# A graph layer's sender rows: 36 of 3224 gathers replaced by row loads on SyncE's queue

## Chip, core, metric

The kernel runs on one core of a Trainium2 chip. The metric is the device time of one execution in microseconds, the median of several. The engines are called PE (TensorE), DVE (VectorE), ACT (ScalarE), POOL (GpSimd) and SP (SyncE) in the profile.

## What is computed

One attention layer of a graph network over 12,500 nodes and 412,500 edges, the edges sorted by receiver:

```
h = max(layernorm(x), 0)
for each edge e from s to d:
    msg_in   = [h[s], h[d], edge_attr[e]]                # 64 + 64 + 32
    message  = silu(msg_in @ W1 + b1) @ W2 + b2
    logit    = silu(msg_in @ Wa1 + ba1) @ Wa2 + ba2
att        = softmax(logit) over all edges
aggregated = sum of att * message by receiver
out        = x + silu([h, aggregated] @ Wu1 + bu1) @ Wu2 + bu2
```

The part that matters here is h[s]: each edge needs a row of its sender, and senders are in no order.

## The kernel before

**Node stage.** The products of h with the sender's and the receiver's part of `[Wa1, W1]` are computed once for each node and stored in HBM as two tables of rows of 128 numbers, 512 bytes each: `ts_d` for senders, `tr_d` for receivers.

**Edge stage (`one_pass`).** The edges are cut into tiles of P = 128, and K = 8 tiles make a group of 1024 edges. There are NG = 403 groups, 3224 tiles. For a group g, `load(g)` does the following:

- eight indirect gathers on GpSimd (line 448), one for each tile: 128 rows of `ts_d`, one to each partition, into `gs`, a tile of 128 x 8 x 128 numbers. The numbers of the senders lie in SBUF in `src_sb`, with an edge's place in its tile as the partition. The pool `gather` has eight buffers of `gs`, so GpSimd can be eight groups ahead.
- for every fourth group (NQ = 4), edge attributes `eo` and receivers `db` for four groups at once, loaded on SyncE's queue (lines 457 and 460), and four window starts read into SyncE's registers (`registers`, line 435, a TENSOR_LOAD).
- two loads on SyncE's queue of the window of receivers' rows (line 467), at an address that comes from such a register. The windows `wins` have three buffers, which the matmuls of line 475 release.
- DVE builds a one-hot matrix of the receivers in `eo` (line 471), and PE multiplies it and the edge attributes with the window (line 475). That gives `pe`, the receivers' and the edges' part.

`begin(g)` adds `gs` to `pe` (line 480, one DVE operation over 128 x 1024) and takes the tanh on ACT (line 481). `end(g)` makes messages and logits of it (lines 491 to 502); some groups later the messages are weighted, summed by receiver and put into `sums`. The order is: `begin(g)`, then `load(g + 2)`, then `end(g)`; the summing of an earlier group is placed between these parts.

A call `pin(...)` keeps an instruction in the program's order on its engine. The DMAs of the edge stage are not pinned; a scheduler places them on their queue, and it adds all semaphores. Between groups 16 and about 120 the bias of the node update is computed along the way (`tile_bias`, `node_bias`, `tile_rest`, lines 310 to 360), which gives SyncE's queue further loads and stores.

**Node update.** After the last group, tiles of 1024 nodes are scaled, passed through the last layers and stored (lines 671 to 745).

The line that the change is about, and the one that consumes its result:

```python
                for j in range(K):
                    nc.gpsimd.indirect_dma_start(
                        out=gs[:, j, :], out_offset=None, in_=ts_d[:, :],
                        in_offset=bass.IndirectOffsetOnAxis(ap=src_sb[:, t + j:t + j + 1], axis=0))
...
                pin(nc.vector.tensor_tensor(gss[g], pes[g], gss[g], ALU.add))
```

Of the kernel before, what the change touches and what calls it, by code (L numbers as in the profile page):

```python
# [44 lines left out]
F32 = mybir.dt.float32  # L45
I32 = mybir.dt.int32
AF = mybir.ActivationFunctionType
ALU = mybir.AluOpType
AX = mybir.AxisListType
ENG = mybir.EngineType  # L50
# [3 lines left out]
P = 128  # L54
# [3 lines left out]
C = 2 * U  # L58
S1 = U + 1
K = 8  # L60
# [8 lines left out]
NQ = 4  # L69
NC = 8  # L70
TABLES = 4
EPS = 1e-5
NEG = -3.0e38
BIG = 3.0e38
# [5 lines left out]
WHY = "a receiver's number; windows past the last node are padded"  # L80


@with_exitstack
def gnn_kernel(ctx: ExitStack, tc: tile.TileContext, n_edges, x, src, dst, dst_row, first, edge,
               weights, out):
    nc = tc.nc
    NB = x.shape[0] // P
    T = src.shape[1]
    NG = T // K
    NP = NB * P  # L90
# [6 lines left out]
    ts_d = dram.tile([NP, C], F32, name="ts_d")  # L97
# [13 lines left out]
    part, at = {}, 0  # L111
# [43 lines left out]
    with tc.tile_pool(name="node1", bufs=1) as node1, \  # L155
# [23 lines left out]
        pin = tc.keep_in_program_order  # L179
# [15 lines left out]
        eps = node1.tile([P, 1], F32, name="eps")  # L195
        nc.vector.memset(eps, EPS)
        pin(nc.scalar.activation(node1.tile([P, 1], F32, name="spare"), eps, AF.Sqrt))
# [90 lines left out]
        for c, nn in chunks:  # L288
            tr = node.tile([P, CB, C], F32, name="tr")[:, :nn, :]
            for b in range(0, nn, 4):  # L290
                n = min(4, nn - b)
                pn = node_ps.tile([P, 4, C], F32, name="pn", bufs=4)
                for i in range(0, n, 2):
# [7 lines left out]
        pin(nc.scalar.dma_start(hT_d, hT))  # L301

    one_pass(tc, n_edges, locals())
    again = nc.values_load(wrong[0:1, 0:1], min_val=0, max_val=1,
                           skip_runtime_bounds_check_because="it is the outcome of a comparison")
# [57 lines left out]
def one_pass(tc, n_edges, v):  # L363
    nc = tc.nc
    NB, T, NG, NP, NT = (v[k] for k in ("NB", "T", "NG", "NP", "NT"))
# [3 lines left out]
    ts_d, tr_d, bq_d, xb_d, edge, dst_row = (  # L369
        v[k] for k in ("ts_d", "tr_d", "bq_d", "xb_d", "edge", "dst_row"))  # L370
# [8 lines left out]
    pin = tc.keep_in_program_order  # L379

    with ExitStack() as ctx:
# [25 lines left out]
        for w in wins:  # L407
            nc.vector.memset(w, 0.0)
            for r in range(2):
                rows = slice(WR + r * DE, WR + (r + 1) * DE)  # L410
                nc.vector.tensor_copy(w[rows, :, r, :], we[rows, None, :].to_broadcast([DE, 2, C]))
        with tc.tile_pool(name="work2", bufs=2) as work2, \
                tc.tile_pool(name="small", bufs=3) as small, \
                tc.tile_pool(name="pre_ps", bufs=AHEAD + 1, space=PSUM) as pre_ps, \
                tc.tile_pool(name="one_ps", bufs=1, space=PSUM) as one_ps:
            pes, gss, lgs, ps_, psums, sps, pps, ees, mts = ({} for _ in range(9))


            w2t_ps = one_ps.tile([P, 4, P], F32, name="mt")[:U, 0, :S1]
# [4 lines left out]
            nc.tensor.matmul(w2u_ps, w2t, wu1a, start=True, stop=True)  # L424
            for h in range(2):
                nc.vector.tensor_copy(w2u[:, h, :], w2u_ps)
            at_sp, at_lo, at_hi, bus = {}, {}, {}, {}


# [3 lines left out]
            def registers(g, engine, at, base=base_sb, top=NP - 1):  # L433
                n = min(NQ, NG - g)
                _, regs = nc.values_load_multi_w_load_instructions(
                    base[0:1, g:g + n], engines=[engine], min_val=0, max_val=top,
                    skip_runtime_bounds_check_because=WHY)
                for i in range(n):
                    at[g + i] = regs[i]

            def load(g):

                t = g * K
                if g % NQ == 0:
                    registers(g, ENG.SP, at_sp)
                gs = gss[g] = gather.tile([P, K, C], F32, name="gs")
                for j in range(K):
                    nc.gpsimd.indirect_dma_start(  # L448
                        out=gs[:, j, :], out_offset=None, in_=ts_d[:, :],
                        in_offset=bass.IndirectOffsetOnAxis(ap=src_sb[:, t + j:t + j + 1], axis=0))  # L450
                if g % NQ == 0:
                    n = min(NQ, NG - g) * E2
                    eo = work2.tile([P, NQ, E2], F32, name="eo")
                    db = work2.tile([WR, NQ, E2], I32, name="db")
                    for i in range(g, min(g + NQ, NG)):
                        ees[i] = eo[:, i - g, :], db[:, i - g, :]
                    nc.sync.dma_start(eo.rearrange("p g e -> p (g e)")[WR:, :n],
                                      edge[:, g * E2:g * E2 + n])
                    for r in range(2):
                        nc.sync.dma_start(  # L460
                            db.rearrange("p g e -> p (g e)")[r * R:(r + 1) * R, :n],
                            bass.AP(tensor=dst_row.tensor, offset=dst_row[r:r + 1, g * E2:].offset,
                                    ap=[[0, R], [1, n]]))
                eo, db = ees.pop(g)
                win = wins[g % WINS]
                for r in range(2):
                    nc.sync.dma_start(win[r * R:(r + 1) * R, :, r, :],
                                      tr_w[bass.ds(at_sp[g], R), :, :])
                for h in range(2):
                    e = slice(h * E2 // 2, (h + 1) * E2 // 2)  # L470
                    pin(nc.vector.tensor_scalar(eo[:WR, e], db[:, e], bj[:, g, h:h + 1], None,  # L471
                                                op0=ALU.is_equal))
                pe = pes[g] = pre_ps.tile([P, K, C], F32, name="pe")
                for q in range(H):
                    pin(nc.tensor.matmul(pe[:, 2 * q:2 * q + 2, :], eo[:, q * P:(q + 1) * P],  # L475
                                         win[:, q // 2, :, :], start=True, stop=True))

            def begin(g):

                pin(nc.vector.tensor_tensor(gss[g], pes[g], gss[g], ALU.add))  # L480
                pin(nc.scalar.activation(pes[g], gss[g], AF.Tanh))  # L481

            def end(g):
# [99 lines left out]
            at, weighed = [None, None], [0]  # L583
# [28 lines left out]
            for g in range(AHEAD):  # L612
                load(g)
            done = 0
            for g in range(NG):
# [3 lines left out]
                if more and g == NG - 1:  # L619
                    next(more)  # L620
                begin(g)
                if more and g < NG - 1:
                    next(more)
# [8 lines left out]
                if g + AHEAD < NG:  # L632
                    load(g + AHEAD)
# [37 lines left out]
        with tc.tile_pool(name="upd1", bufs=1) as upd1, \  # L671
# [12 lines left out]
                                         engines=[ENG.SP, ENG.DVE, ENG.PE, ENG.Activation])  # L684
# [63 lines left out]
def general(tc, n_edges, v, dst):  # L748
# [7 lines left out]
    with ExitStack() as ctx:  # L756
        keep = ctx.enter_context(tc.tile_pool(name="keep_g", bufs=1))
        act_d = dram.tile([P, T, S1], F32, name="act_d")
        sum_d = [dram.tile([NP + P, S1], F32, name=f"sum_d{r}") for r in range(TABLES)]
        before = keep.tile([P, P], F32, name="before")  # L760
# [15 lines left out]
        rows = (NP + P) // P  # L776
        for r in range(TABLES):
            flat = sum_d[r].rearrange("(p b) f -> p (b f)", p=P)
# [66 lines left out]
        with tc.tile_pool(name="sums_g", bufs=2) as work, \  # L845
                tc.tile_pool(name="sums_g_ps", bufs=2, space=PSUM) as sums_ps:
            for g in range(0, T, G):
# [3 lines left out]
                for k in range(0, ng, K):  # L851
# [26 lines left out]
                    for j in range(K):  # L878
                        nc.gpsimd.indirect_dma_start(
                            out=sum_d[(t + j) % TABLES][:, :],  # L880
                            out_offset=bass.IndirectOffsetOnAxis(ap=to[:, j:j + 1], axis=0),
# [6 lines left out]
        with tc.tile_pool(name="upd_g", bufs=2) as work, \  # L888
                tc.tile_pool(name="upd_g_ps", bufs=2, space=PSUM) as upd_ps:
            for c in range(0, NB, CB):  # L890
                part = work.tile([P, TABLES, CB, S1], F32, name="part")
                for r in range(TABLES):
                    nc.sync.dma_start(part[:, r], sum_v[r][:, c:c + CB, :])
                for r in range(1, TABLES):
                    nc.vector.tensor_tensor(part[:, 0], part[:, 0], part[:, r], ALU.add)
# [95 lines left out]
```

## Time and profile before

| What | Value |
|---|---|
| median of 3 runs | 4154.89 us (4154.44 to 4157.52) |
| profiled execution, device time | 4154.71 us |
| its span, first to last instruction | 4153.0 us |
| granted TensorE clock, mean | 0.638 of full speed |
| first gather starts / last gather ends | 50.8 us / 4082.75 us |
| DMA queue of GpSimd: packets, MB, share of 16 engines | 103168, 211.49, 20.4% |
| DMA queue of SyncE: packets, MB, share of 16 engines | 107538, 168.42, 15.4% |

The profile shows one execution. A group line gives the source line, the engine, the operation, output and inputs with shapes and the count; then the total busy time in us and the mean duration in ns; then the idle time of the engine just before these instructions, and what ended most of it. "issue" is time in which the engine waited for nothing that the profile shows. The line of tenths cuts the span into 40 slices; a digit is the busy share of that slice, so 7 is 70%. A timeline line starts with the start and the length in us. SPq is SyncE's queue: its instructions issue DMAs and don't count as busy.

### The profile page before, as it was taken

What the parts mean: (1) busy time and instruction counts of PE and PEld (TensorE: products, weight loads), DVE (VectorE), ACT (ScalarE), POOL (GpSimd) and SP (SyncE); (2) the same over time, 40 slices, a digit from 0 to 9 for tenths busy, and PEclk for the clock granted to TensorE, in tenths of its full rate; (3) what the DMA queues carried; (4) which work ended last, traced back from release to release, by engine and by line L of the source; (5) the groups of instructions that cost most, each with busy time, mean ns of one, the idle gap of its engine ahead of it and who ended that gap; (6) DMA issues with size and microseconds to landing.
All of it is one profiled execution on the core that took longest, in us unless ns stands there. A gap on an engine that the chain in (4) does not pass through costs nothing.

```text
span 4153.0 us, 45361 instructions
## 1 busy us (share of the span) xinstructions
PE 2227.8 (54%) x10980; PEld 1802.9 (43%) x10980; DVE 2986.2 (72%) x8482; ACT 584.9 (14%) x1235; POOL 3065.0 (74%) x3249
## 2 busy tenths in 40 slices
PE   5555554545555555545555555555554555655555
PEld 4433443434444444444444444444443444444445
DVE  6867776767677677776777767777677776777777
ACT  3211111111111111111111111111111111111112
POOL 3777777777777777777777777777777777777773
PEclk8666666766666556666666666666666566556665
DMA  7433343434333333333333333333333333333323
GB/s 276 109 86 96 98 102 97 102 92 107 97 90 88 90 81 90 83 87 90 80 90 83 88 90 80 90 82 88 90 80 90 82 88 90 81 90 82 88 77 112
DMA packets 212354, 392.54 MB, mean 95 GB/s; under 512 B 73009, under 2 KB 137842, under 8 KB 198898
## 3 DMA queue, kind: packets, MB, share of 16 engines
q0 software_dynamic: 103168, 211.49, 20.4%
q1 hardware_dynamic: 107538, 168.42, 15.4%
q10 hardware_dynamic: 1376, 9.67, 0.6%
q8 instruction: 90, 1.47, 0.1%
q14 instruction: 182, 1.49, 0.1%
HBM read 363.56 MB, written 25.72 MB: 94 GB/s over the span
## 4 chain that ended last, share of the span: by engine, by line


## 5 line engine op out<-in xcount | busy, mean ns | idle before, releaser
L448 POOL DMA_INDIRECT gs<-ts_d,src_sb x3224 | 3047.9, 945 | 1032.5 <-issue 932.2
L475 PE MATMUL pe<-wins,eo 128*128 128x256 f32 x3224 | 1421.7, 616 | 1080.7 <-DVE eo L471 953.5
L475 PEld LDWEIGHTS pe<-wins,eo 128*128 128x128 f32 x3224 | 954.6, 311 | 1370.9 <-DVE eo L471 1025.2
L480 DVE TENSOR_TENSOR gs<-pe,gs 128x1024 f32<-128x1024 f32 x403 | 491.6, 1220 | 942.5 <-DMA gs<-ts_d,src_sb 932.1
L481 ACT ACTIVATE pe<-gs 128x1024 f32<-128x1024 f32 x403 | 413.9, 1027 | 2487.2 <-DVE gs L480 1776.1
L543 DVE TENSOR_SCALAR wt<-iota_w,dloc,p 128x40 f32<-128x40 f32 x3224 | 719.1, 316 | 0.1
L549 PE MATMUL sp<-wt,acts 128*65 128x40 f32 x6448 | 608.4, 267 | 0.7 <-DVE wt L543 0.7
L549 PEld LDWEIGHTS sp<-wt,acts 128*65 128x65 f32 x6448 | 578.6, 183 | 1.1 <-DVE wt L543 0.8
L560 PEld LDWEIGHTS mt<-ss,w2u 65*128 65x128 f32 x806 | 221.4, 289 | 495.9 <-issue 446.6
L560 PE MATMUL mt<-ss,w2u 65*128 65x40 f32 x806 | 184.9, 324 | 386.0 <-DVE gm L526 381.3
L499 DVE TENSOR_TENSOR pe<-pe,w_all 128x512 f32<-128x512 f32 x403 | 281.6, 699 | 12.6
L491 DVE SCALAR_TENSOR_TENSOR acts<-pe,gs 128x512 f32<-128x512 f32 x403 | 277.7, 689 | 15.5 <-ACT pe L481 5.2
L497 DVE SCALAR_TENSOR_TENSOR pe<-pe,gs 128x512 f32<-128x512 f32 x403 | 280.2, 695 | 10.9
L471 DVE TENSOR_SCALAR eo<-db,bj 64x256 f32<-64x256 int32 x806 | 280.0, 379 | 7.6
L502 DVE TENSOR_REDUCE lg<-pe 128x8 f32<-128x512 f32 x403 | 276.5, 686 | 8.9
L519 PE MATMUL mt<-ident,mx 128*128 128x128 f32 x103 | 44.8, 435 | 409.4 <-DVE sums L577 360.6
L519 PEld LDWEIGHTS mt<-ident,mx 128*128 128x128 f32 x103 | 18.3, 178 | 420.1 <-issue 417.7
L579 DVE COPY stand<-nmax 64x40 f32 x806 | 151.5, 188 | 2.0
L530 ACT ACTIVATE scale<-fall 128x1 f32<-128x1 f32 x103 | 20.9, 203 | 804.8 <-DVE fall L529 804.8
L577 DVE TENSOR_TENSOR sums<-sums,mt 64x40 f32 x600 | 113.4, 189 | 28.7 <-PE mt L560 24.0
L555 ACT COPY ss<-sp 65x40 f32<-65x40 f32 x403 | 73.6, 183 | 21.4 <-PE sp L549 20.4
L573 DVE SCALAR_TENSOR_TENSOR sums<-sums,scale,mt 64x40 f32 x206 | 52.4, 254 | 33.2 <-PE sp L549 23.3
(91 smaller groups left out, 565.4 us busy)
## 6 DMA issues: line engine op xcount, KB each, us to landing
gs<-ts_d,src_sb POOLq DMA_INDIRECT x3224
eo<-in_edge_dram SPq DMA_DIRECT2D x100, 512.0 KB
db<-in_dst_row_dram SPq DMA_DIRECT2D x200, 256.0 KB
wins<-tr_d SPq DMA_DIRECT2D x806, 32.0 KB
ts_d<-ts SPq DMA_DIRECT2D x5, 896.0 KB
tr_d<-tr ACTq DMA_DIRECT2D x5, 896.0 KB
hT_d<-hT ACTq DMA_DIRECT2D x1, 3136.0 KB
hb<-hT_d SPq DMA_DIRECT2D x48, 64.0 KB
```

Source lines behind the costliest of these rows:

```text
L448: nc.gpsimd.indirect_dma_start(out=gs[:, j, :], out_offset=None, in_=ts_d[:, :], in_offset=bass.IndirectOffsetOnAxis(ap=src_sb[:, t + j:t ...
L471: pin(nc.vector.tensor_scalar(eo[:WR, e], db[:, e], bj[:, g, h:h + 1], None, op0=ALU.is_equal))
L475: pin(nc.tensor.matmul(pe[:, 2 * q:2 * q + 2, :], eo[:, q * P:(q + 1) * P], win[:, q // 2, :, :], start=True, stop=True))
L480: pin(nc.vector.tensor_tensor(gss[g], pes[g], gss[g], ALU.add))
L481: pin(nc.scalar.activation(pes[g], gss[g], AF.Tanh))
L491: pin(nc.vector.scalar_tensor_tensor(acts[g % ACTS][:, :, 0:U], th[:, :, U:C], 1.0, gs[:, :, U:C], op0=ALU.add, op1=ALU.mult))
L497: pin(nc.vector.scalar_tensor_tensor(att, th[:, :, 0:U], 1.0, gs[:, :, 0:U], op0=ALU.add, op1=ALU.mult))
L499: pin(nc.vector.tensor_tensor(att, att, wa2[:, None, :].to_broadcast([P, K, U]), ALU.mult))
L502: pin(nc.vector.tensor_reduce(lgs[s][:, k:k + K], att, AX.X, ALU.add))
L543: pin(nc.vector.tensor_scalar(wt[:, j, :], iota_w[:, j // H, :], dloc[:, g * K + j:g * K + j + 1], p[:, k + j:k + j + 1], op0=ALU.is_equal ...
L549: pin(nc.tensor.matmul(sp, acts[g % ACTS][:, j, :], wt[:, j, :], start=j == 0, stop=j == K - 1))
L560: pin(nc.tensor.matmul(pp, w2u.rearrange("s h u -> s (h u)"), sps.pop(g), start=True, stop=True))
```

## The change

On 36 groups (11, 22, up to 396) GpSimd gathers seven tiles rather than eight. The eighth tile's 128 rows are fetched one by one, as 128 plain loads of 512 bytes on SyncE's queue, into a tile of their own, `alone[g]` (two buffers). Twelve rows are issued in each of the eleven `load` steps ahead of the group (eight in the last). The row numbers come from a new input, `src_row`, the list of senders as one row in HBM: 128 of them are loaded to one partition (`numbers`), and twelve are read into SyncE's registers in each step. In `begin` the add for such a group is made in two operations, over 128 x 896 and over 128 x 128.

```diff
+QUEUES = [(ENG.SP, 11, 0, 12)]
...
+            rows_at, rows_to = {}, {}
+            dma = {ENG.SP: nc.sync, ENG.Activation: nc.scalar}
+
+            def numbers(q, g):
+
+                if g < NG - 4:
+                    t = g * K + K - 1
+                    rows_at[q, g] = small.tile([1, P], I32, name=f"one_src{q}", bufs=2)
+                    nc.sync.dma_start(rows_at[q, g], v["src_row"][:, t * P:(t + 1) * P])
+
+            def rows(q, g):
+                engine, every, phase, n_rows = QUEUES[q]
+                if g == 0:
+                    numbers(q, phase + every)
+                if g < phase:
+                    return
+                at = (g - phase) % every
+                g = g - at + every
+                if at == 0:
+                    rows_at.pop((q, g - every), None)
+                    if (q, g) in rows_at:
+                        alone[g] = work2.tile([P, C], F32, name=f"one_gs{q}")
+                if at == every // 2:
+                    numbers(q, g + every)
+                if (q, g) not in rows_at:
+                    return
+                a = at * n_rows
+                n = min(n_rows, P - a)
+                if n <= 0:
+                    return
+                load, regs = nc.values_load_multi_w_load_instructions(
+                    rows_at[q, g][0:1, a:a + n], engines=[engine], min_val=0, max_val=NP - 1,
+                    skip_runtime_bounds_check_because=WHY)
+                for k in range(n):
+                    dma[engine].dma_start(alone[g][a + k:a + k + 1, :], ts_d[bass.ds(regs[k], 1), :])
...
@@ load(g)
-                for j in range(K):
+                for j in range(K - (g in alone)):
                     nc.gpsimd.indirect_dma_start(
...
                                       tr_w[bass.ds(at_sp[g], R), :, :])
+                for q in range(len(QUEUES)):
+                    if QUEUES[q][0] == ENG.SP:
+                        rows(q, g)
...
@@ begin(g)
-                pin(nc.vector.tensor_tensor(gss[g], pes[g], gss[g], ALU.add))
+                n = K - (g in alone)
+                pin(nc.vector.tensor_tensor(gss[g][:, :n, :], pes[g][:, :n, :], gss[g][:, :n, :], ALU.add))
+                if n < K:
+                    pin(nc.vector.tensor_tensor(gss[g][:, n, :], pes[g][:, n, :], alone.pop(g), ALU.add))
                 pin(nc.scalar.activation(pes[g], gss[g], AF.Tanh))
...
+        "src_row": padded(src, t * P)[None],
```

More of the change, by code (lines that the diff above doesn't have):

```diff
@@ L83, in gnn_kernel @@
 @with_exitstack
-def gnn_kernel(ctx: ExitStack, tc: tile.TileContext, n_edges, x, src, dst, dst_row, first, edge,
+def gnn_kernel(ctx: ExitStack, tc: tile.TileContext, n_edges, x, src, src_row, dst, dst_row, first, edge,
                weights, out):
@@ L415, in one_pass @@
                 tc.tile_pool(name="one_ps", bufs=1, space=PSUM) as one_ps:
-            pes, gss, lgs, ps_, psums, sps, pps, ees, mts = ({} for _ in range(9))
+            pes, gss, lgs, ps_, psums, sps, pps, ees, mts, alone = ({} for _ in range(10))
             w2t_ps = one_ps.tile([P, 4, P], F32, name="mt")[:U, 0, :S1]
```

## The prediction

> **What bounds the kernel now.** I read the busy shares first, then the costliest groups, then the waits of GpSimd alone between 130 and 4083 us, then the timeline at the end of the gathers. The busy shares leave it open (VectorE 72%, GpSimd 74%); the group lines begin to decide.
>
> ```profile
> PE 2227.8 (54%) x10980; PEld 1802.9 (43%) x10980; DVE 2986.2 (72%) x8482; ACT 584.9 (14%) x1235; POOL 3065.0 (74%) x3249
> ...
> POOL 3777777777777777777777777777777777777773
> ...
> L448 POOL DMA_INDIRECT gs<-ts_d,src_sb x3224 | 3047.9, 945 | 1032.5 <-issue 932.2
> ...
> L480 DVE TENSOR_TENSOR gs<-pe,gs 128x1024 f32<-128x1024 f32 x403 | 491.6, 1220 | 942.5 <-DMA gs<-ts_d,src_sb 932.1
> ```
>
> 3224 gathers of 945 ns, each with a gap ahead of it that is put down to "issue", which is a wait for nothing. VectorE's idle time is nearly all at L480, waiting for the gathers to land. The waits of GpSimd (what it waited for, us in total, times, longest) say that no other engine holds it up:
>
> ```profile
> POOL gs L448 <- issue: 867.3, 2846, 0.3
> POOL gs L448 <- DVE eo L471: 32.0, 105, 0.3
> POOL gs L448 <- DMA gs<-ts_d,src_sb: 31.4, 103, 0.3
> POOL gs L448 <- DVE gs L480: 18.6, 61, 0.3
> ```
>
> The longest is 0.3 us, the ordinary gap, whoever is named as releaser. So after the start GpSimd never waits for a buffer: it runs at its own pace. The timeline gives that pace and its end:
>
> ```profile
> 4080.56 0.94 POOL L448 DMA_INDIRECT gs<-ts_d,src_sb  x1 [0.30 <-issue]
> 4081.81 0.94 POOL L448 DMA_INDIRECT gs<-ts_d,src_sb  x1 [0.30 <-issue]
> 4106.60 1.26 POOL L710 TENSOR_TENSOR uT<-uT,bu_in 128x512 f32<-128x512 f32 x1 [23.84 <-DVE uT L705]
> ```
>
> One gather every 1.249 us (median start to start over the whole trace; the mean from the first at 50.8 to the last at 4081.8 is 1.251). A group of eight takes 9.99 us. The last gather ends at 4082.75, and 70.25 us of tail follow to 4153.0.
>
> The other queue that matters is SyncE's, which is to carry the new work: its waits in total, then the durations (ns, min/median/max) of the two lines that resemble the new instructions, and one pair in the timeline.
>
> ```profile
> SPq L467 <- PE mt L560: 1266.4, 199, 12.4
> SPq L467 <- PE pe L475: 800.9, 107, 10.4
> SPq L460 <- DVE wt L543: 748.3, 97, 18.9
> SPq L467 <- PE sp L549: 458.8, 94, 11.8
> ...
> L435 SPq TENSOR_LOAD <-base_sb x101: 294/298/1808, 78.8 to 4013.5; - x101
> ...
> L467 SPq DMA_DIRECT2D wins<-tr_d x806: 316/317/1368, 86.3 to 4041.0; - x162
> ...
> 1992.32 0.82 SPq L467 DMA_DIRECT2D wins<-tr_d  x2
> ```
>
> SyncE waits about 3270 us of the span in these four lines alone, mostly for one of the three window buffers to come free. Two window loads take 0.82 us from first start to second end; less 0.317, a load with a register in its address costs 0.50 us start to start, address arithmetic included.
>
> **What the Trainium skill says.** "DMA: Bandwidth & Descriptors", section "Issuing engines are not separate DMA queues": DMAs from SyncE, ScalarE and GpSimd end on the same 16 engines, and spreading them saves only the issuing sequencer's time. That time is exactly what is short here: the two main queues take 20.4% and 15.4% of the 16 engines, while GpSimd issues without a pause. The same page, "Why a DMA increments its semaphore by 16 and not by 1", advises one semaphore for each transfer in flight. The trace agrees: SyncE's loads rotate over eight semaphores, and the records show each load waiting for the one eight before it to land. Its "Latency and other measured facts" puts a tensor_load at some 600 ns at least; here four registers take 298 ns, and the measurement decides.
>
> **Removed.** Targets are groups 11, 22, ... 396: the list of senders is fetched only for a group below NG - 4 = 399, so there are 36, as the title says. Each drops one gather: 36 x 1.249 = 45.0 us of GpSimd's time. All of it lies on the path, since GpSimd never pauses for 0.3 us or more between 130 us and its end. Unless something below becomes late, its last gather moves from 4082.75 to 4037.8, and the tail (unchanged code) with it.
>
> **Added on SyncE.** One turn of 11 groups lasts 11 x 9.99 = 109.9 us before and 108.7 us with one gather fewer. Into it go 128 row loads and 11 register loads, plus one 512-byte list load.
> - A row load: 0.50 us, as a window load, since it also takes its address from a register. Lower end 0.36 us (317 ns and its 45 ns gap, arithmetic free); upper end 0.65, since the strided loads of L318 and L355 take 598 and 656 ns (medians). I take 0.50: a row is simpler than a window, 512 bytes rather than 32 KB. 128 x 0.50 = 64 us.
> - A register load: 12 numbers rather than 4. At best one of 0.35 us (298 ns and its gap), at worst three; 11 x 0.35 = 4 us, up to 12. The list load 0.4 us.
> - What SyncE does already: per group two window loads (1.0 us), a quarter of the eo, db and register loads (0.43), and on average 0.2 for the node bias, with semaphore instructions some 1.85 us (704 us active between 200 and 4000 us, summed from the records). 11 x 1.85 = 20 us.
> - Rotation of semaphores: eight rows back is 4.0 us at 0.50 each. A window load lands 1.75 us after issue (median from the records), so rows don't wait for rows; an eo load lands after 5.0 us and a db load after 3.9 (6.1 in the slowest tenth), so a row eight behind one waits 1 to 2 us, three times in four groups at most: up to 7 us a turn.
>
> Sum: 64 + 4 + 0.4 + 20 + 7 = 95 us of 108.7; with three register loads 103. SyncE fits, at 88 to 95%.
>
> **What is queued behind the rows.** The rows of a step stand after that step's two window loads, so the next windows come up to 6 us later, and behind them the matmul L475, then L480. What covers this: from the records a window load is issued 25.9 us (median; 17.4 at the fifth percentile) ahead of its matmul, eo 47.9 us ahead. And because SyncE runs ahead of TensorE by the three buffers and mostly waits for it, the rows fill that wait rather than add to it. If SyncE is late for longer, VectorE gets late; GpSimd still has eight gather buffers, some 60 us, before it stops. The register loads stayed behind the window loads of the preceding group in the records, so I expect the rows to keep their place too, and not to be drawn forward in one burst of 128. The densest stretch is 200 to 1250 us, where the node bias adds 0.7 us per group instead of 0.2: about 100 us a turn, near the limit, but the slack covers it.
>
> At the start, step 0 loads its list and waits for it on SyncE (some 2 us), then issues 12 rows (6 us) ahead of the second window. GpSimd starts at 50.8 and VectorE's first add is at 98.5, so five groups of lead cover that: nothing.
>
> **Added on VectorE.** The add of 128x1024 (1220 ns) becomes 128x896 and 128x128. Rows of those shapes take 1093 (L231) and 281 ns (L728): +0.15 us, and up to four more semaphore instructions of 50 ns since the rows came on eight semaphores: 0.35 x 36 = 13 us. VectorE waits 932 us for gathers, so this costs nothing; without that cover it would cost the 13 us. The rows' landing is no new wait: the last eight rows are issued with the step before the target's own window, more than 17 us ahead of the target's matmul.
>
> **Added on the DMA engines.** 4608 rows of 512 bytes, 2.4 MB beside 392.5 MB. If each is cut in 16, that is 74,000 packets beside 212,354: perhaps 10% more of engines that are a third busy. Gathers may land a little later; their pace is GpSimd's, so nothing.
>
> **Sum.** 4154.71 (this execution; span 4153.0 and 1.7 around it) - 45.0 = 4109.7; the median of the runs, 4154.89, is 0.2 above this execution. Forecast 4110 us.
>
> **The rivals.**
> - Partly lost (4118 to 4146, as a point 4130): in the dense stretch SyncE falls behind for longer than the slack, windows come late, and VectorE stalls until the stretch is over. For it: 100 of 108.7 us there, and SyncE's own waits in order (it waits for the x transfer and VectorE's add before L360). Against: VectorE needs 7.2 busy us per group of 9.96 and catches up. Chance 0.07.
> - No change (4155): VectorE is really what paces, in bursts. For it: pairs of groups without a pause. Against: GpSimd's waits never exceed 0.3 us. 0.02.
> - Slower: SyncE becomes the bound. It decides from the row price at which its turn exceeds 109.9 us: (109.9 - 20.4 - 4.3) / 128 = 0.67 us, or 0.61 if the semaphore waits come to 7 us. At 0.70 us a turn takes 20.4 + 4.3 + 89.6 = 114.3, so 36 x 4.4 = 158 us more: 4313. For it: no load of one row is in the trace, twelve in a row follow each other without a pause, which no line of SyncE does now, and loads at L318 cost 0.6. Against: those move 64 partitions in several runs, and the second of a window pair costs 317 ns like the first. 0.11.
>
> **How the numbers follow.** The main case has 0.80, most of it between 4104 and 4118; the spread being the few us by which the end of the groups and the tail can fall differently. With the lower part of the partial case, 4104 to 4132 holds 8 in 10. A measurement here can tell about 0.2%, 8.3 us, from no change: faster 0.86 (main, nearly all of the partial case), same 0.03, slower 0.11.
>
> **What would show it.** Right: 3188 gathers at the same 1.249 us with no wait of GpSimd over 0.3 us, the last ending near 4038, a tail of 70 us, rows about 0.50 us apart, SyncE still waiting at L467. Wrong: matmuls at L475 waiting for windows, GpSimd waiting for VectorE at a group's start, rows over 0.6 us apart, or a longer gap between gathers.

## The result, and the profile after

| | before | changed |
|---|---|---|
| median, us | 4155.69 (4 runs) | 4114.97 (4 runs) |
| ratio, 95% interval | | 0.9902 (0.9885 to 0.9919) |
| profiled execution, span | 4153.0 | 4113.8 |
| gathers | 3224 | 3188 |
| last gather ends, then tail | 4082.75, 70.2 | 4043.2, 70.6 |

The kernel before took 4152 to 4158 us beside most of the runs below and 4155 to 4167 us beside four of them, so every run is compared, by ratio, with the kernel before that ran beside it.

The change gains 40.7 us by the medians and 39.2 us between the two profiled spans; the forecast was 45.0 us and 4110 us, with a range of 4104 to 4132. The page's lines for GpSimd and for two VectorE groups after the change, and then the second of these groups before it:

```profile
POOL 3777777777777777777777777777777777777773
...
L487 POOL DMA_INDIRECT gs<-ts_d,src_sb x3188 | 3018.7, 947 | 1022.1 <-issue 952.1
...
L523 DVE TENSOR_TENSOR gs<-pe,gs 128x1024 f32<-128x1024 f32 (+1 forms) x403 | 487.7, 1211 | 775.5 <-DMA gs<-ts_d,src_sb 740.0
...
L513 DVE TENSOR_SCALAR eo<-db,bj 64x256 f32<-64x256 int32 x806 | 259.7, 360 | 158.6 <-DMA db<-in_dst_row_dram 151.5
```

```profile
L471 DVE TENSOR_SCALAR eo<-db,bj 64x256 f32<-64x256 int32 x806 | 280.0, 379 | 7.6
```

GpSimd still sets the pace, with 36 gathers fewer, and a mean gather of 947 rather than 945 ns. VectorE waits less for gathers (740 us against 932), but it has a new wait: 151.5 us for `db`, whose loads stand in SyncE's queue (before, all idle time at that line was 7.6 us). The three largest waits of GpSimd between 130 and 4044 us say that this reaches it nowhere:

```profile
POOL gs L487 <- issue: 887.3, 2910, 0.3
POOL gs L487 <- DMA gs<-ts_d,src_sb: 14.0, 46, 0.3
POOL gs L487 <- DVE eo L513: 14.0, 46, 0.3
```

As before, no wait is longer than 0.3 us. SyncE's side: its waits, the durations (ns, min/median/max) of the new register loads, and a stretch of its timeline.

```profile
SPq L506 <- PE pe L517: 291.7, 69, 9.9
SPq L506 <- PE mt L605: 256.1, 138, 10.8
SPq L506 <- PE sp L594: 99.0, 84, 5.2
...
SPq L464 <- DMA db<-in_dst_row_dram: 88.9, 118, 1.4
```

```profile
L460 SPq TENSOR_LOAD <-one_src x396: 527/933/1367, 88.6 to 3933.3; - x198
```

```profile
2014.12 0.86 SPq L506 DMA_DIRECT2D wins<-tr_d  x2
2016.15 4.82 SPq L464 DMA_DIRECT2D one_gs<-ts_d  x12
2021.88 0.86 SPq L506 DMA_DIRECT2D wins<-tr_d  x2
```

At the window loads, some 2530 us of waiting before have shrunk to 650 at L506; the 748 us before that for the buffers of `db` are nearly gone too (24.9 us, now at L496). Between the window pair and the first row lies the register load of 0.93 us; twelve rows take 4.82 us, 0.41 us from one to the next (median). In the records SyncE is active for 79% of the time between 200 and 4000 us. Active means here, and below, its instructions with the gaps between them, where a gap is no longer than 0.4 us.

### The profile page after: what moved, and what is told of

Same layout as the page of the kernel before. It is cut to its first block, busy times and chain, and to the rows that moved or that the text cites. A ratio compares the mean times of both kernels' runs of the same rounds, so it can differ in the third digit from the quotient of the medians.

```text
span 4113.8 us, 59789 instructions
## 1 busy us (share of the span) xinstructions
PE 2284.8 (56%) x10980; PEld 1852.9 (45%) x10980; DVE 3021.4 (73%) x8518; ACT 584.3 (14%) x1235; POOL 3035.8 (74%) x3213
## 2 busy tenths in 40 slices
DMA packets 220602, 393.50 MB, mean 96 GB/s; under 512 B 77077, under 2 KB 146554, under 8 KB 207034
## 4 chain that ended last, share of the span: by engine, by line
## 5 line engine op out<-in xcount | busy, mean ns | idle before, releaser
L517 PE MATMUL pe<-wins,eo 128*128 128x256 f32 x3224 | 1477.3, 638 | 967.7 <-DVE eo L513 819.6
L517 PEld LDWEIGHTS pe<-wins,eo 128*128 128x128 f32 x3224 | 1000.5, 325 | 1265.8 <-DVE eo L513 970.2
L523 DVE TENSOR_TENSOR gs<-pe,gs 128x1024 f32<-128x1024 f32 (+1 forms) x403 | 487.7, 1211 | 775.5 <-DMA gs<-ts_d,src_sb 740.0
L588 DVE TENSOR_SCALAR wt<-iota_w,dloc,p 128x40 f32<-128x40 f32 x3224 | 734.0, 320 | 0.1
L513 DVE TENSOR_SCALAR eo<-db,bj 64x256 f32<-64x256 int32 x806 | 259.7, 360 | 158.6 <-DMA db<-in_dst_row_dram 151.5
L624 DVE COPY stand<-nmax 64x40 f32 x806 | 163.4, 203 | 0.6
```

The costliest lines, as they stand in the source:

```text
L523: pin(nc.vector.tensor_tensor(gss[g][:, :n, :], pes[g][:, :n, :], gss[g][:, :n, :], ALU.add))
L588: pin(nc.vector.tensor_scalar(wt[:, j, :], iota_w[:, j // H, :], dloc[:, g * K + j:g * K + j + 1], p[:, k + j:k + j + 1], op0=ALU.is_equal ...
```

## The experiments

### Is the gain the gathers, and are the rows free?

**Gathers dropped, no rows** (the 36 tiles' sender rows and the loads of their numbers are left out; the add takes zeros).

```diff
...
-                    if (q, g) in rows_at:
-                        alone[g] = work2.tile([P, C], F32, name=f"one_gs{q}")
+                    if g < NG - 4:
+                        alone[g] = v["zero"]
...
-                if (q, g) not in rows_at:
-                    return
+                return
```

> The 36 eighth gathers are left out and nobody fetches these rows: the add takes zeros for them, in the same two VectorE operations; no row load, no list load. Theory A (the gain is GpSimd's pace times the gathers removed, and the rows are hidden on SyncE; the 5 us that the changed kernel lacks come from gathers that are stretched now and then while VectorE works, whoever fetches the rows): 4155.7 - 36 x 1.25 = 4110.7, with up to 5 us more if gathers are stretched here too, so 4111 to 4116, within 0.15% of the changed kernel. Rival B (the rows' traffic or SyncE's lateness costs the 5 us): 4110 to 4111 with no more stretched gathers than in the kernel before, and a clear 4 to 5 us below the changed kernel.

**Rows loaded, gathers kept** (the eighth gather's result is overwritten by the second add).

```diff
-                for j in range(K - (g in alone)):
+                for j in range(K):
```

> The rows are loaded as in the changed kernel and added as there, but GpSimd gathers all eight tiles too (its eighth result is overwritten by the add). Theory A: as before, 4155 to 4160, GpSimd at 1.25 us per gather, no wait over 0.3 us. Rival B (rows slow the gathers by traffic): 4160 to 4162. Rival of the forecast (SyncE sets the pace with these rows): clearly slower than before, over 4170.

**The changed kernel once more.**

> The changed kernel once more, on the same chip as the two above. 4112 to 4117; a repeat of the profile should again show some 70 gathers of over 960 ns if these are fixed by the program's order, and another number if they are chance.

| Run | ratio to before | interval | span of the profiled execution | gathers over 960 ns |
|---|---|---|---|---|
| gathers dropped | 0.9906 | 0.9891 to 0.9921 | 4113.5 | 68 |
| rows, gathers kept | 1.0007 | 0.9999 to 1.0015 | 4165.7 | 59 |
| changed again | 0.9901 | 0.9886 to 0.9917 | 4113.1 | 77 |

The kernel without the rows is not faster than the one with them, and the rows without the saving cost at most 0.15%. So the gain is the dropped gathers, and 4608 row loads are hidden, in this amount. Rival B falls: the 5 us are missing where no row is loaded, too. So does the forecast's rival of no change: VectorE does not set the pace, since fewer gathers alone give the gain. The span of the second run is longer mostly because all of GpSimd ran at a median of 1.252 us from gather to gather in that execution, rather than 1.249; the kernel before was slower beside it, too.

### Where the missing 5 us are

From the records, gathers over 960 ns exceed the usual 944 by 5.5 us in all in the kernel before (60 gathers) and by 9.6 us in the changed kernel (72); the rest of the shortfall is spread thinly over the pace. Of the long ones in the changed kernel, 23 start at the same place in VectorE's order (26 in its repeat). One of them in the timeline:

```profile
2729.55 0.60 DVE L513 TENSOR_SCALAR eo<-db,bj 64x256 f32<-64x256 int32 x2
2729.83 1.19 POOL L487 DMA_INDIRECT gs<-ts_d,src_sb  x1 [0.30 <-issue]
...
2730.08 0.20 DVE L651 SCALAR_TENSOR_TENSOR total<-total,scale,psum 128x1 f32<-128x1 f32 x1
2730.21 1.76 DVE L588 TENSOR_SCALAR wt<-iota_w,dloc,p 128x40 f32<-128x40 f32 x8
```

The gather takes 1.19 us instead of 0.94; it starts with the second L513, and the add to `total` and the building of `wt` follow. Before the change there were only four in that place. So this place alone makes 4.6 us of the difference. Two runs move that add behind the building of `wt`, in the changed kernel and in the kernel before:

```diff
+                    by_node(g)
                     if g == starts[s]:
                         pin(nc.vector.scalar_tensor_tensor(total, total, scale[:, s:s + 1],
                                                            psums.pop(s), op0=ALU.mult, op1=ALU.add))
-                    by_node(g)
```

> The changed kernel with VectorE's addition to total (128x1) placed behind the eight operations that build wt, instead of ahead of them, in the first group of each batch. Theory S (gathers are stretched by about 0.24 us where they begin with a fixed run of VectorE operations, total among them): the gathers over 960 ns in that place vanish or change in number, 4 to 6 us at most, ratio 0.989. Rival (stretching has nothing to do with VectorE's order): again 20 to 30 such gathers and the same time.

> The kernel before, without the change, with the addition to total behind the building of wt. Theory S: before the change few gathers met that run (four or five, 1 us in all), since groups and gathers stood in one fixed phase; so 1 us at most, ratio 0.999 to 1.000. If it gains 5 us here too, what the order of total brings has nothing to do with the change.

The changed kernel goes to 0.9887 (0.9872 to 0.9902), its profiled span to 4104.7. Its gather line in the groups:

```profile
L487 POOL DMA_INDIRECT gs<-ts_d,src_sb x3188 | 3010.9, 944 | 1022.1 <-issue 927.5 <-DMA gs<-ts_d,src_sb 50.9 <-DVE gs L523 13.1
```

The mean is 944 ns; 24 gathers exceed 960 ns, none of them in that place, and the busy time falls by 7.8 us, a little more than the 4 to 6 us that were expected at most. The kernel before stays at 0.9994 (0.9986 to 1.0003). The two ratios of the changed kernel overlap in their intervals; what shows the effect is the gathers themselves. Within the changed kernel, too, the records hold a comparison: of the gathers that start less than 25 ns after a second L513, 23 of 28 are long where the add to `total` follows, and none of 63 where `wt` follows at once; with the add moved, none of 80. So this loss comes from VectorE's order meeting the gathers.

Why the change brings them together is open in part. Before, the add to `total` mostly stands at one place in the gathers' rhythm: 58 of 100 adds start 1.22 to 1.25 us after the last gather's start, 4 start 0.23 to 0.27 us after it, which is the bad place. In the changed kernel it is 27 and 28. Groups with seven gathers would shift this rhythm, but they can't be the whole reason: the run with the rows and all eight gathers has 25 adds in the bad place, and 24 long gathers there. That run and the one with the gathers dropped (31 long gathers there) have in common the add made in two operations, which makes VectorE's order longer in 36 groups; no run has that alone.

Why this run of instructions holds a gather is argued only: the Trainium skill, "SBUF — State Buffer", section "SBUF: two separate sides", says that a VectorE operation in a mode that uses both of its ports locks GpSimd out of the shared pair, so that it cannot write descriptors, and "Who interferes with whom" counts tensor_scalar among the operations that can enter such a mode. L513 and L588 are tensor_scalar, though no trace here shows their mode; and of the 838 gathers that overlap an L588 in the changed kernel, 775 take 960 ns or less. So the page gives a direction, not the case.

### How far SyncE can carry it

**44 tiles, 15 rows per step**, the same code with other numbers:

```diff
-QUEUES = [(ENG.SP, 11, 0, 12)]
+QUEUES = [(ENG.SP, 9, 0, 15)]
```

> Every ninth group, 15 rows per step, 44 tiles rather than 36. SyncE's sum for a turn of nine groups: 128 rows x 0.412 + 128 registers x 0.08 + 9 x 1.85 + 1 = 81 us, with waits for semaphores some 85, against 88.7 us that GpSimd takes. Theory A: it still fits, 4155.7 - 44 x 1.25 + 5 = 4106. Rival (SyncE near its limit already costs, and more rows give part of it back): 4115 or above, with matmuls waiting for windows.

Ratio 1.0893 (1.0878 to 1.0908): slower by 370 us, far beyond theory A's 4106 us and beyond what its rival had in mind (4115 or above). The waits and the register load of this run:

```profile
DVE eo L513 <- DMA db<-in_dst_row_dram: 1032.1, 97, 22.0
...
PE pe L517 <- DMA wins<-tr_d: 773.4, 164, 12.7
```

```profile
L460 SPq TENSOR_LOAD <-one_src x396: 531/3178/3667, 88.4 to 4378.1; - x198
```

VectorE and TensorE wait for loads of SyncE's queue, and SyncE is active for 99% of the time from 1300 to 4000 us. The surprise is the register load: 3.18 us in the median for 15 numbers, against 0.93 for 12. Split by step, it takes 3.26 us, but 1.55 and 1.64 us in the two of these steps whose first number lies at 0 and 60, multiples of four. (The ninth step reads the last 8 numbers, from 120, in 0.71 us.) Two runs separate the count from the start:

**44 tiles, 16 rows per step**, so that each start is a multiple of 16: `(ENG.SP, 9, 0, 16)`.

> Every ninth group again, 44 tiles, but 16 rows per step (8 steps with rows, the ninth without), so every register load starts at a multiple of 16 numbers. Theory L (the run with 15 rows was slow because of its register loads alone: 3.26 us where the first number lay at no multiple of four, 1.6 us where it did, against 0.93 for 12 numbers): a register load of 16 takes 1.2 to 1.6 us, SyncE's turn sums to 53 (rows) + 8 x 1.3 + 17 + 1 = 81 us of 88.7, GpSimd sets the pace again: ratio to before 0.987 to 0.989, 10 us faster than the changed kernel. Rival N (it is the number of rows per turn or loads of more than 12 numbers as such): register loads of 3 us again, ratio over 1.03.

**The changed kernel with its list one number further on**, 12 numbers per load as before:

```diff
-                    rows_at[q, g] = small.tile([1, P], I32, name=f"one_src{q}", bufs=2)
+                    rows_at[q, g] = small.tile([1, P + 4], I32, name=f"one_src{q}", bufs=2)[:, 1:P + 1]
```

> The changed kernel with its list of 128 row numbers stored one number further on in SBUF, so that no register load starts at a multiple of four numbers; 12 numbers per load as before. Theory L (the start decides): a register load takes 2.6 us or so rather than 0.93, SyncE's turn grows by 11 x 1.7 = 18 us to some 104 of 108.7, so the stretch of the node bias overflows and the gain is partly or wholly lost: ratio 0.995 to 1.02. Rival (the count of 15 did it): 0.93 us as before and ratio 0.990.

The register loads of the two, in this order:

```profile
L460 SPq TENSOR_LOAD <-one_src x352: 973/1157/1602, 89.0 to 3962.5; - x176
```

```profile
L460 SPq TENSOR_LOAD <-one_src x396: 1673/2654/3082, 88.9 to 3999.9; - x198
```

16 numbers from a start at a multiple of four take 1.16 us, 12 from one number further on 2.65. The start decides, as theory L has it. And it decides the result: the changed kernel with nothing but this shift is slower than before, 1.0065 (1.0050 to 1.0081).

The other half of theory L's expectation for the 44 tiles failed: 1.0003 (0.9995 to 1.0011), no gain. Where that went is shown by the waits of GpSimd, first from 200 to 1400 us, then from 1400 to 4000 us:

```profile
POOL gs L487 <- issue: 301.4, 836, 7.7
```

```profile
POOL gs L487 <- issue: 571.4, 1874, 0.3
```

In the first stretch, the one with the node bias, there are waits of up to 7.7 us (named "issue": the profile shows no releaser); after it none over the usual 0.3. In the records GpSimd falls 48 us behind its pace from 600 to 1400 us, and 5 us from there to 3800. So SyncE's queue overflows there, and only there. It is active for some 91% of that stretch. The rest is nearly all waits of its own, and 81 of their 111 us are at the two stores of this side job (lines 342 and 362), for ScalarE's copy, VectorE's add and a transfer:

```profile
SPq L342 <- ACT bu L339: 46.2, 13, 6.4
...
SPq L362 <- DVE hb L361: 20.5, 13, 5.4
SPq L362 <- DMA hb<-in_x_dram: 14.7, 13, 1.5
```

While it waits there, the rows and windows behind it in the queue wait too. Spreading the node bias tests whether the bunching is the cause:

```diff
-                if g >= 16 and g // 8 - 2 < NT:
-                    c = (g // 8 - 2) * NC
-                    if g % 8 in (1, 5):
-                        tile_bias(tc, c, g % 8 == 1, v, work2, one_ps, bus)
-                    elif g % 8 == 3:
+                if g >= 16 and (g - 16) // 24 < NT:
+                    c, r = (g - 16) // 24 * NC, (g - 16) % 24
+                    if r in (1, 13):
+                        tile_bias(tc, c, r == 1, v, work2, one_ps, bus)
+                    elif r == 7:
```

> The version with every ninth group and 16 rows per step (44 tiles), with the node bias spread over groups 16 to 328, one tile of nodes in 24 groups rather than in 8. Theory D (that version gained nothing because SyncE's queue overflowed in the stretch of the node bias alone, by 50 us up to 1400 us, and was in balance after it): the overflow goes, all 44 gathers are gained, pauses of GpSimd of at most 5 us in all, ratio 0.987 to 0.990. Rival (SyncE at over 90% is too slow everywhere, and the bias only moves its share): pauses of 30 us or more, now over the whole of it, ratio 0.995 or above.

0.9896 (0.9881 to 0.9912): the overflow is gone, and GpSimd's longest wait after 130 us is 0.3 us again:

```profile
POOL gs L487 <- issue: 880.5, 2888, 0.3
```

Its ratio is no better than that of 36 tiles, though: 118 gathers are over 960 ns, with 13.6 us of excess, and the tail is 3 us longer. With the add to `total` moved as well:

> The same, and the addition to total behind the building of wt. If both theories hold, 44 x 1.25 = 55 us less, and none of the 5 us of stretched gathers: ratio 0.986 to 0.988, faster than all kernels so far. If the spread fails, as the version without it.

0.9875 (0.9860 to 0.9891), a median of 4103.26 us: the lowest of all, and the version to keep, though its interval overlaps that of the 36 tiles with the same order (0.9887). 52 gathers are long, 4.2 us in all.

**49 tiles**, `(ENG.SP, 8, 0, 16)`, for the other end:

> Every eighth group, 16 rows per step, 49 tiles. The point from which the slower rival decides: rows 53 + register loads 8 x 1.3 + present work 15 + 1 = 79.5 us plus waits for semaphores, against 78.7 us of GpSimd. SyncE sets the pace: no gain over the version with every ninth group, between ratio 0.99 and 1.03, VectorE and TensorE waiting for windows and db. If it came out at 0.985 instead, SyncE's price per turn is lower than the sum says.

1.0369 (1.0353 to 1.0385), above the range: SyncE is active for 98% of the time from 1300 to 3900 us, and GpSimd falls 137 us behind up to 1400 us and 33 more to 3800.

### A second queue

17 further tiles on ScalarE's queue, beside the 36:

```diff
-QUEUES = [(ENG.SP, 11, 0, 12)]
+QUEUES = [(ENG.SP, 11, 0, 12), (ENG.Activation, 22, 5, 8)]
...
-                    if QUEUES[q][0] == ENG.SP:
-                        rows(q, g)
+                    rows(q, g)
```

> The changed kernel, and beside it every 22nd group's last tile (27, 49, up to 379: 17 tiles) fetched in the same manner on ScalarE's queue, 8 rows per step for 16 of 22 steps. Theory A: 53 gathers fewer, 4155.7 - 53 x 1.25 + 5 = 4094 in the first session's terms, ratio 0.985, if ScalarE's rows (some 4 us per group beside 1.5 us of activations) find idle time. Rival W (the rows stand in ScalarE's queue ahead of the tanh, the copy of the sums or the exponentials, and VectorE waits for these): no better than the changed kernel, ratio 0.990 or above, VectorE's waits for ScalarE growing from a few us to over 100.

0.9891 (0.9876 to 0.9906): not theory A's 0.985, and not to be told from the changed kernel's 0.9902 by the intervals. The 17 gathers are worth 21 us; the profiled span falls by 10.6. VectorE's waits of this run (its line numbers from L507 on are lower by one):

```profile
DVE eo L512 <- DMA db<-in_dst_row_dram: 619.1, 78, 14.9
...
DVE acts L535 <- ACT pe L525: 7.5, 4, 3.4
```

VectorE doesn't wait for ScalarE (7.5 us at the tanh), against rival W. It waits for `db`, four times as long as without the second queue, and in the stretch of the node bias GpSimd loses another 7 us. SyncE's own waits show why its loads come later:

```profile
SPq L464 <- DMA one_gs<-ts_d: 307.8, 205, 14.8
SPq L499 <- DMA one_gs<-ts_d: 109.4, 47, 5.4
SPq L506 <- DMA one_gs<-ts_d: 68.8, 34, 5.6
```

In the changed kernel SyncE has next to no wait for a row. Here the loads of both queues take their semaphores from the same eight, in rotation, so a load of SyncE can stand behind a row that ScalarE's queue has yet to issue. By the records SyncE waits 434 us at loads whose semaphore was last used by a row of ScalarE, 231 times, 14.8 us at most. A kernel with semaphores of its own for each queue wasn't tried, so what the second queue would give without this stays open.

## Why the prediction was right

- **Gathers removed.** 36 x 1.249 us were on the path, as forecast; dropping them without rows and with them gives the same ratio. GpSimd's last gather came at 4043.2, not 4037.8, and the tail was 70.6 us for 70.25.
- **The term that was mis-sized** is GpSimd's pace, taken as a constant 1.249 us, and "their pace is GpSimd's, so nothing". The mean from gather to gather rose from 1.2507 to 1.2525 us, 5.8 us over 3187 steps. The forecast named transfers as the only thing that could touch a gather; it was VectorE's order, at 4.6 us of the 5.8, and the run with another order has 1.2500 us.
- **Price of a row.** 0.41 us, within the bounds of 0.36 and 0.65, below the 0.50 taken. A register load of 12 numbers took 0.93 us, near the worst case of three loads. The two errors go against each other: 128 x 0.412 + 11 x 0.99 (with the gap) = 64 us for the 68 forecast. SyncE's earlier work, put at 704 us, comes to 658 us by the count used here, 19 us a turn for 20. In all, SyncE's 79% of 108.7 us is 86 us, for a forecast of 95.
- **Luck.** Steps of twelve rows put every register load at a multiple of four numbers. The forecast did not ask for this, and one number further on the same change loses (1.0065).
- **What covers the rows.** The lead of window loads over their matmuls, 25.9 us before, stayed at 25.6 us (median) after group 140 but sank to about 5 us from group 0 to 120. "The slack covers it" holds, but nearly all of it was used, and VectorE waited 129.5 us for `db` between 200 and 1400 us. What kept GpSimd going is the second cover that was named, its buffers.
- **The partly-lost rival** is real. It stood eight tiles away: with 44 tiles the stretch of the node bias takes 50 us, as its mechanism says.
- **The slower rival** is real as well, but its deciding point was put in the wrong place: not a row's price of 0.61 to 0.67 us, but the register load. The bounds of 0.35 to 1.05 us for it left out where its first number lies, and a start one number further on alone makes the change a loss.
- **VectorE's split add** cost nothing by its own length, as forecast: the waits for gathers covered it. Whether it moved the add to `total` onto the bad place is open, as said above.
- **The DMA engines.** 220602 packets for 212354: a row wasn't cut in 16, and the added packets didn't matter.

## What to carry to other kernels

Here, work on an engine that never waits was worth its full pace, and another queue could take it over so long as that queue's sum, its waits for others counted in, stayed below the pace in the densest stretch, not on average: with 44 tiles the queue was active for 91% of the time between 200 and 4000 us and overflowed where a side job was bunched, and it fitted at 92% once that job was spread. The queue that shared its semaphores with a second one also took over that one's delays. Before the last few per cent are moved, price each kind of instruction in the queue by itself, with its alignment; register loads that were an eighth of the queue's active time decided between a gain of 1% and a loss. When an engine's fixed pace is the bound, look for single long instructions in it: the order of another engine can lengthen them.

## What the runs showed of the hardware that was not expected

- A TENSOR_LOAD on SyncE takes, in the medians by step, 0.71 us for 8 numbers, 0.93 for 12 and 1.16 for 16 when the first lies at a multiple of four; 1.85 us for 8, 2.65 for 12 and 3.26 for 15 when it doesn't; 1.55 for 15 from an aligned start. This fits some 0.25 us, and 0.22 us for each aligned four or 0.20 us for each single number, 15 from an aligned start being three fours and three singles, and all numbers from another start being singles. That is a fit to these runs. It isn't the whole: the older load of four numbers at L435 took 298 ns before and 488 ns in the changed kernel, where it is L474. The 600 ns that the Trainium skill gives as a floor ("DMA: Bandwidth & Descriptors", "Latency and other measured facts") aren't one here: both of these lie below it.
- A load of one row with a register in its address takes 228 ns to issue, for 317 (before) and 334 ns (after) of a window of 32 partitions, and in the records it lands 1.40 us after its issue starts (medians).
- A gather is lengthened by 0.24 us at one place in VectorE's order (23 of the 28 that start there in the changed kernel), and not where the same instructions follow without the 128x1 add (none of 63).
- With one set of semaphores for two queues, row loads on ScalarE's queue held up SyncE's loads by up to 14.8 us.
